# A graph-attention and mixture-of-experts layer: the vector a loaded as two rows and spread by a product with ones, and six products on constants at the start

## The chip, the cores and the metric

The kernel runs on one core of a Trainium2 chip. The metric is the time of one execution on the device in microseconds (us), median over several executions. A core has five engines with an instruction queue each: TensorE (PE; its weight loads are shown apart as PEld), VectorE (DVE), ScalarE (ACT), GpSimd (POOL) and SyncE (SP). SP here only issues DMA transfers; ACT issues two at the start. All transfers share 16 DMA engines.

## What is computed

One layer on x of 3327 x 256, padded to 3328 rows: graph attention with 4 heads of 64 columns over a random adjacency matrix, then a mixture of 16 experts of which each row takes two. Cut to what matters here:

```
h = (layernorm(x) @ W).reshape(n, 4, 64)
a1, a2 = a[:64, 0], a[64:, 0]
s = einsum('nhd,d->nh', h, a1 + a2)
e = where(adj[:, None, :] > 0, leaky_relu(s)[:, :, None], -9e15)
h' = einsum('nhm,mhd->nhd', softmax(e), h)
x = x + layernorm(h') * gamma + beta
x = x + mixture_of_experts(layernorm(x))
```

The vector `a` has 128 values, and it is used through the sum of its two halves alone.

## The kernel before

**Score columns.** The scores s are linear in the rows of h, so four columns are put in front of W: `w_sb` has `H + D` = 260 columns, the first four being W of each head times `a1 + a2`, summed over the 64 columns. `score_columns` makes them on VectorE: `a_sum` from the two halves of `a_bc` (L457), the product `ha` with W (L459), and the sums (L461). `a_bc` is `a` broadcast to all 128 partitions by a DMA on ScalarE's queue (`row_broadcast`, L222, called at L242). W follows on the same queue (L244).

**Centring.** The layer norm's mean is taken out of W in place of x: `center` multiplies W by a constant matrix `mean` on TensorE (L447) and subtracts the result on VectorE (L450), once for the 256 columns of W, once for the four score columns.

**The h stage.** The 26 row tiles (128 rows each) are in seven groups (`SIZES`). For each tile `h_stage` takes statistics of x on VectorE (L492, L493), the root on GpSimd (L497, L498), turns the tile by two transposes on TensorE (L473), copies it on ScalarE (L476, tile `xnt`), multiplies it by `w_sb` (L481), and splits the result into a high part on ScalarE (`hi`, L484) and a low part on VectorE (`lo`, L487). Group 0 is loaded in four tiles, the others group by group (`load_x`, L240).

**The masks.** Blocks of the adjacency matrix of up to 512 x 512 are loaded (`sg`, L561), turned into ones and zeros on VectorE (`mk`, L564) and multiplied with hi and lo on TensorE (L587, L588). There are three buffers for blocks and three for masks.

**After that** each group is finished (softmax terms, layer norms, routing), and the experts work on gathered rows (L959, L974, L985), whose results are added to the output (L988).

**The order.** Nearly all work is given to `plan`. Each `plan.add` names an engine, an assumed cost in us, a rank, what it comes after, the buffers that it uses, and for a load an assumed time to landing and a size. `Plan.run` makes 80 orders by a greedy choice (the work that can start earliest by the assumed times, then the rank), replays each with random variations of the costs, and emits the one with the smallest total. Every engine then works in that order. What stands above the plan in the code (constants, the loads of `a` and W) is emitted first, in the order of the code. PSUM buffers are named by a kind and the rest of a key: the kinds `pt` and `ph` have two buffers each, and a new key waits for the users of the key two before it.

The works that open the plan are at L1080 to L1089: four loads of x tiles, the landing of W (a work without an instruction), `score_columns`, and the two centrings.

Of the kernel before, what the change touches and what calls it, by code (L numbers as in the profile page):

```python
# [47 lines left out]
F32 = mybir.dt.float32  # L48
# [6 lines left out]
P = 128  # L55
# [3 lines left out]
D = 256  # L59
H = 4  # L60
DH = 64
# [15 lines left out]
CAP = 512  # L77
# [137 lines left out]
def gnn_moe(ctx: ExitStack, tc: tile.TileContext, x, adj_t, W, a, gamma, beta, gate_w, gate_b, w1, w2, w3, out):  # L215
    nc = tc.nc

    const = ctx.enter_context(tc.tile_pool(name="const", bufs=1))

    def row_broadcast(ap, size, name):  # L220
        t = const.tile([P, size], F32, name=name)
        nc.scalar.dma_start(t, bass.AP(tensor=ap.tensor, offset=ap.offset, ap=[[0, P], [1, size]]))  # L222
        return t


    XF = [const.tile([P, len(tiles), ROW], F32, name=f"x{g}") for g, tiles in enumerate(GROUPS)]
    X = [t[:, :, :D] for t in XF]
# [2 lines left out]
    def row_of(t):  # L230

        return (t + FIRST) % NT * P
# [5 lines left out]
    def load_x(g, t0, t1):  # L238
        r0 = row_of(GROUPS[g][0]) + t0 * P
        nc.sync.dma_start(X[g][:, t0:t1, :], x[r0:r0 + (t1 - t0) * P, :].rearrange("(t p) d -> p t d", p=P))  # L240

    a_bc = row_broadcast(a, 2 * DH, "a_bc")  # L242
    w_sb = const.tile([P, KC, H + D], F32, name="w_sb")
    nc.scalar.dma_start(w_sb[:, :, H:], W.rearrange("(k p) d -> p k d", p=P))  # L244
    gamma_bc = const.tile([P, D], F32, name="gamma_bc")
# [12 lines left out]
    ones = const.tile([P, P], BF, name="ones")  # L258
# [5 lines left out]
    warm = const.tile([P, 1], F32, name="warm")  # L264
# [72 lines left out]
    tiny = ctx.enter_context(tc.tile_pool(name="tiny", bufs=2))  # L337
# [10 lines left out]
    PE, DVE, ACT, POOL, SP = "PE", "DVE", "ACT", "POOL", "SP"  # L348
# [51 lines left out]
    plan = Plan(SLOTS, take)  # L400
# [7 lines left out]
    def psum(key):  # L408
        return T[key]
# [31 lines left out]
    SPLIT, LOADED = {}, {}  # L441
# [11 lines left out]
        return means, subtract  # L453

    def score_columns():
        a_sum = tiny.tile([P, DH], F32, name="a_sum", bufs=1)
        nc.vector.tensor_add(a_sum, a_bc[:, :DH], a_bc[:, DH:])  # L457
        ha = work.tile([P, KC, H, DH], F32, name="ha", bufs=1)
        nc.vector.tensor_tensor(ha, w_sb[:, :, H:].rearrange("p k (h d) -> p k h d", h=H),  # L459
                                a_sum[:, None, None, :].to_broadcast([P, KC, H, DH]), op=ALU.mult)  # L460
        nc.vector.tensor_reduce(w_sb[:, :, :H], ha, AX.X, ALU.add)  # L461
# [615 lines left out]

    for t in range(GT):  # L1080
        LOADED[0, t] = plan.add(SP, 0.6, (0, t), [], lambda t=t: load_x(0, t, t + 1), landing=2.0, size=P * D * 4)

    landed = plan.add(SP, 0.0, (0, 0), [], lambda: None, landing=2.5, size=D * D * 4)
    summed = plan.add(DVE, 1.6, (0,), [landed], score_columns)
    SCORES = []
    for made, c0, c1, c in ((landed, H, H + D, 1.0), (summed, 0, H, 0.5)):
        means, subtract = center(w_sb, ("ph", "w", c0), c0, c1)
# [4 lines left out]
    for step in range(NG):  # L1092
        if step + 1 < NG:
            g = step + 1
            LOADED[g] = plan.add(SP, 0.6, (1, step - 0.5), [], lambda g=g: load_x(g, 0, len(GROUPS[g])), landing=2.0,
                                 size=len(GROUPS[g]) * P * D * 4)
# [46 lines left out]
    size = 3 * D * HID * 4  # L1143
# [22 lines left out]
    with tc.If(many["value"] > 0):  # L1166
        with tc.For_i(0, NL) as i:
# [4 lines left out]
            with tc.For_i(0, full * (NT // AGAIN)) as c:  # L1172
# [12 lines left out]
                for k in range(KC):  # L1185
                    pt = ps_tr.tile([P, CAP], F32, name="pt")
# [51 lines left out]
```

## Time and profile before

| | us |
|---|---|
| median of 3 runs | 533.23 (532.13 to 533.85) |
| the profiled execution | 530.4 |
| its span, first to last instruction | 528.7 |
| VectorE starts on x | 5.37 |
| first product with W (L481) starts | 10.91 |
| first mask product (L587) starts | 14.77 |
| last product (L985) is done | 522.7 |

All times in the text are from the start of the span. DMA issues are on the queue of the engine that issues them (ACTq, SPq): the time shown there is the issuing, not the transfer. From 5 to 30 us the DMA engines move 317 to 386 GB/s, and nearly nothing from 31 to 45 us. From 15 us to 200 us PE shows no idle time. A group of instructions in the trace is shown with its start, its whole length and its count; matmuls are pipelined, so a group's length over its count comes nearer to what one costs than a single one's shown duration.

### The profile page before, as it was taken

To read this page: it belongs to the slowest core of one execution; us is meant where nothing else is said; L and a number is where in the kernel's file an instruction comes from. 1 tells how busy PE (TensorE), PEld (TensorE's weight loads), DVE (VectorE), ACT (ScalarE), POOL (GpSimd) and SP (SyncE) were. 2 spreads that over 40 slices of the span, in tenths; PEclk is the share of its full clock that TensorE was granted. 3 is DMA by queue.
4 is the path that set the end of the run, shared out by engine and by line. 5 is a ranking of instruction groups with operands and counts; after the bars stand their busy time and mean duration, and the time that the engine had idled before them with its cause. 6 is when DMAs were issued, how large, how long until landed. Compare 5 with 4: busy or idle time off the path is not lost. (4 is left out here: it accounts for less than half of the span.)

```text
span 528.7 us, 8608 instructions
## 1 busy us (share of the span) xinstructions
PE 513.8 (97%) x2997; PEld 406.5 (77%) x2998; DVE 274.5 (52%) x848; ACT 161.2 (30%) x464; POOL 213.0 (40%) x240
## 2 busy tenths in 40 slices
PE   5999999999999999999899999999999999999995
PEld 4889999999999999777687557566566756666673
DVE  4978564876869799678822222222233233423221
ACT  2562153636372750565222211201211121112110
POOL 4230022121031411756676555364465546622333
PEclk9999999999999999999999999999999999999999
DMA  7932889797879895554649544463465545543222
GB/s 269 366 128 75 304 261 300 247 338 230 273 212 360 271 374 168 184 153 136 173 83 304 150 96 125 107 147 116 112 143 154 136 111 140 152 109 68 30 29 28
DMA packets 63534, 94.69 MB, mean 179 GB/s; under 512 B 4858, under 2 KB 36990, under 8 KB 63488
## 3 DMA queue, kind: packets, MB, share of 16 engines
q1 hardware_dynamic: 52304, 80.04, 46.2%
q0 software_dynamic: 10768, 13.75, 15.3%
q8 instruction: 24, 0.39, 0.3%
q10 hardware_dynamic: 416, 0.33, 0.2%
q14 instruction: 22, 0.18, 0.1%
HBM read 81.61 MB, written 13.90 MB: 181 GB/s over the span
## 5 line engine op out<-in xcount | busy, mean ns | idle before, releaser
L587 PE MATMUL pa<-hi,mk 128*128 128x258 f32 x676 | 167.6, 289 | 0.0
L588 PE MATMUL pa<-lo,mk 128*128 128x256 f32 x676 | 163.2, 281 | 0.0
L587 PEld LDWEIGHTS pa<-hi,mk 128*128 128x128 f32 x676 | 127.7, 189 | 1.1 <-issue 1.0
L588 PEld LDWEIGHTS pa<-lo,mk 128*128 128x128 f32 x676 | 127.5, 189 | 0.1
L988 POOL DMA_INDIRECT out<-y,out_index x61 | 94.0, 1541 | 60.7 <-DVE y L1068 38.9
L974 PE MATMUL pa<-xt,w1e 128*128 128x400 f32 (+8 forms) x272 | 98.6, 485 | 0.0
L974 PE MATMUL pa<-xt,w2e 128*128 128x400 f32 (+8 forms) x272 | 98.0, 483 | 0.0
L1050 DVE TENSOR_TENSOR hid<-s,pa 128x400 f32<-128x400 f32 (+9 forms) x76 | 40.3, 530 | 109.2 <-PE pa L974 89.2
L959 POOL DMA_INDIRECT x<-normed,index x61 | 64.1, 1050 | 81.3 <-PE pt L1030 59.0
L1047 ACT ACTIVATE s<-pa 128x400 f32<-128x400 f32 (+9 forms) x76 | 35.8, 472 | 196.9 <-PE pa L974 196.9
L985 PE MATMUL ph<-w3e,hid 128*128 128x256 f32 (+2 forms) x400 | 89.4, 379 | 0.0
L985 PEld LDWEIGHTS ph<-w3e,hid 128*128 128x128 f32 (+2 forms) x400 | 73.7, 188 | 10.4
L974 PEld LDWEIGHTS pa<-xt,w2e 128*128 128x128 f32 x272 | 49.5, 190 | 36.9 <-issue 18.0
L974 PEld LDWEIGHTS pa<-xt,w1e 128*128 128x128 f32 x272 | 49.2, 190 | 35.7 <-issue 19.8
L564 DVE TENSOR_SCALAR mk<-sg 128x2048 fp32r<-128x2048 f32 (+2 forms) x49 | 54.2, 1107 | 28.6 <-PE pa L588 28.6
L1068 DVE TENSOR_SCALAR y<-ph,weight 128x256 f32<-128x256 f32 (+5 forms) x54 | 26.0, 482 | 70.5 <-PE ph L985 64.2
L653 POOL TENSOR_TENSOR hp<-csum,c 128x512 f32<-128x512 f32 (+1 forms) x14 | 15.1, 1097 | 65.0 <-DVE c L649 65.0
L481 PE MATMUL ph<-w_sb,xnt 128*128 128x260 f32 x104 | 27.6, 401 | 0.0
L1037 ACT COPY xt<-pt 128x512 f32<-128x512 f32 (+2 forms) x38 | 17.4, 504 | 19.4 <-PE pt L1030 19.4
L481 PEld LDWEIGHTS ph<-w_sb,xnt 128*128 128x128 f32 x104 | 18.2, 193 | 4.0 <-issue 1.2
L423 POOL TENSOR_SCALAR rs_x<-spread_x 128x4 f32<-128x4 f32 (+1 forms) x7 | 1.8, 259 | 47.4 <-ACT pay L429 44.3
L667 ACT ACTIVATE agg<-agg,c 128x64 f32<-128x64 f32 x76 | 18.8, 336 | 1.9 <-DVE c L649 1.8
(177 smaller groups left out, 466.3 us busy)
## 6 DMA issues: line engine op xcount, KB each, us to landing
sg<-in_adj_t SPq DMA_DIRECT2D x25, 1024.0 KB, 6.1
sg<-in_adj_t SPq DMA_DIRECT2D x20, 768.0 KB, 5.0
w1e<-in_ffn_w SPq DMA_DIRECT2D x15, 512.0 KB, 3.3
w2e<-in_ffn_w SPq DMA_DIRECT2D x15, 512.0 KB, 4.4
w3e<-in_ffn_w SPq DMA_DIRECT2D x15, 512.0 KB, 4.5
normed<-pay SPq DMA_DIRECT2D x5, 520.0 KB, 6.6
out<-x SPq DMA_DIRECT2D x5, 512.0 KB, 5.6
sg<-in_adj_t SPq DMA_DIRECT2D x4, 576.0 KB, 4.6
```

Source lines behind the costliest of these rows:

```text
L481: nc.tensor.matmul(ph[:, :H + D], T["xnt", g, t][:, k, :], w_sb[:, k, :], start=(k == 0), stop=(k == KC - 1))
L564: nc.vector.tensor_scalar(T[mk][:, :m, :n * P], T[sk][:, :m, :n * P], 0.0, None, op0=ALU.is_gt)
L587: nc.tensor.matmul(pa[:, :D + 2], lhs, HI[mg][:, i, H:], start=first, stop=False)
L588: nc.tensor.matmul(pa[:, :D], lhs, LO[mg][:, i, H:], start=False, stop=left[g, t] == 0)
L667: nc.scalar.mul(at, at, some("c")[:, 0, t, h:h + 1])
L959: nc.gpsimd.indirect_dma_start(out=xe[:, t, :], out_offset=None, in_=normed[:limit], in_offset=at_rows(idx, t), bounds_check=limit - 1, oo ...
L974: nc.tensor.matmul(p[:, :n], wt[:, k, j * P:(j + 1) * P], xt[:, k, :n], start=(k == 0), stop=(k == KC - 1))
L985: nc.tensor.matmul(py[:m, :D], hid[:, j, t * P:t * P + m], w3e[:, j, :], start=(j == 0), stop=(j == JC - 1))
L988: i = nc.gpsimd.indirect_dma_start(out=out, out_offset=at_rows(idx, t, m), in_=y[:m], in_offset=None, bounds_check=NP - 1, oob_is_err=Fals ...
L1047: nc.scalar.activation(T["gate", i, j][:, :n], psum(key)[:, :n], AF.Silu)
L1050: nc.vector.tensor_mul(hid()[:, j, :n], T["gate", i, j][:, :n], psum(key)[:, :n])
L1068: nc.vector.tensor_scalar(T[yk][:mm], psum(key)[:mm, :D], weight, None, op0=ALU.mult)
```

## The change

The broadcast load of `a` goes. In its place SP loads `a` as two rows of 64 values, `a_rows`, just after the first tile of x, and a product of a `[2, 128]` tile of ones, `two`, with `a_rows` puts the sum of both halves into all 128 partitions of a PSUM tile (`("ph", "a")`). `score_columns` reads that tile; its addition goes. Before everything else on TensorE stands `warm_up`: six products of the constant bf16 tile `ones` with itself, repeated to 512 columns, into a `pt` tile that nobody reads. The planned costs of the first x loads go from 0.6 to 0.45, and that of `score_columns` from 1.6 to 1.4.

```
-    def row_broadcast(ap, size, name):
-        t = const.tile([P, size], F32, name=name)
-        nc.scalar.dma_start(t, bass.AP(tensor=ap.tensor, offset=ap.offset, ap=[[0, P], [1, size]]))
-        return t
...
-    a_bc = row_broadcast(a, 2 * DH, "a_bc")
+    a_rows = const.tile([2, DH], F32, name="a_rows")
+    two = const.tile([2, P], F32, name="two")
+    nc.vector.memset(two, 1.0)
...
     def score_columns():
-        a_sum = tiny.tile([P, DH], F32, name="a_sum", bufs=1)
-        nc.vector.tensor_add(a_sum, a_bc[:, :DH], a_bc[:, DH:])
+        a_sum = psum(("ph", "a"))[:, :DH]
...
+    def warm_up():
+        for _ in range(6):
+            nc.tensor.matmul(psum(("pt", "warm")), ones, ones[:, None, :].to_broadcast([P, CAP // P, P]), start=True, stop=True)
+
+    plan.add(PE, 2.2, (0, -1), [], warm_up, [("pt", "warm")])
     for t in range(GT):
-        LOADED[0, t] = plan.add(SP, 0.6, (0, t), [], lambda t=t: load_x(0, t, t + 1), landing=2.0, size=P * D * 4)
+        LOADED[0, t] = plan.add(SP, 0.45, (0, t), [], lambda t=t: load_x(0, t, t + 1), landing=2.0, size=P * D * 4)
+        if t == 0:
+            got = plan.add(SP, 0.45, (0, t), [], lambda: nc.sync.dma_start(
+                a_rows, bass.AP(tensor=a.tensor, offset=a.offset, ap=[[DH, 2], [1, DH]])), landing=2.0, size=512)
+
+    spread = plan.add(PE, 0.2, (0,), [got], lambda: nc.tensor.matmul(psum(("ph", "a"))[:, :DH], two, a_rows, start=True, stop=True),
+                      [("ph", "a")])
 
     landed = plan.add(SP, 0.0, (0, 0), [], lambda: None, landing=2.5, size=D * D * 4)
-    summed = plan.add(DVE, 1.6, (0,), [landed], score_columns)
+    summed = plan.add(DVE, 1.4, (0,), [landed, spread], score_columns, [("ph", "a")])
```

## The prediction

> **What bounds the kernel now.** The page comes first: its busy times, and the span cut into slices of 13.2 us.
>
> ```profile
> PE 513.8 (97%) x2997; PEld 406.5 (77%) x2998; DVE 274.5 (52%) x848; ACT 161.2 (30%) x464; POOL 213.0 (40%) x240
> PE   5999999999999999999899999999999999999995
> PEclk9999999999999999999999999999999999999999
> ```
>
> PE is busy nearly throughout, and only the first and the last slice hold half a slice of idle time. So a microsecond by which PE begins its stream sooner, or runs it faster, moves the end unless a new wait eats it. The PEclk digits cannot show a slow clock inside the first slice.
>
> Second, the waits of PE over the whole span (total us, times, longest):
>
> ```profile
> PE pt L473 <- DMA x<-in_x: 5.5, 1, 5.5
> PE pt L1030 <- DMA x<-normed,index: 1.4, 1, 1.4
> PE ph L447 <- DMA w_sb<-in_gnn_W: 0.9, 1, 0.9
> ```
>
> Two of the three large ones are at the start: for the first tile of x, then for W. Nothing large stands between there and 262 us, where the 1.4 us are.
>
> Third, PE in order of time from 5 to 24 us (start, length of the group, line, tiles, count):
>
> ```profile
> 5.48 0.66 PE L473 MATMUL pt<-ident,x 128*128 128x128 f32 x2 [5.48 <-DMA x<-in_x]
> 7.05 2.05 PE L447 MATMUL ph<-w_sb,mean 128*128 128x256 f32 x4 [0.91 <-DMA w_sb<-in_gnn_W]
> 8.89 1.06 PE L473 MATMUL pt<-ident,x 128*128 128x128 f32 x4
> 9.74 0.85 PE L447 MATMUL ph<-w_sb,mean 128*128 128x4 f32 x4
> 10.91 2.44 PE L481 MATMUL ph<-w_sb,xnt 128*128 128x260 f32 x8
> ...
> 17.26 0.60 PE L473 MATMUL pt<-ident,x 128*128 128x128 f32 x4
> ...
> 19.88 2.02 PE L481 MATMUL ph<-w_sb,xnt 128*128 128x260 f32 x8
> ```
>
> Compare like with like. Four transposes take 1.06 us at 8.89 and 0.60 at 17.26. A 256-column f32 product takes 0.51 at 7.05 (2.05 over 4), a 260-column one 0.25 at 19.88 (2.02 over 8), and the eight at 10.91 are in between. TensorE runs its first work at half speed and speeds up during the eight products that begin at 10.91.
>
> Fourth, ScalarE's queue and VectorE over the same stretch:
>
> ```profile
> 0.83 0.40 ACTq L222 DMA_DIRECT2D a_bc<-in_gnn_a  x1
> 1.27 0.46 ACTq L244 DMA_DIRECT2D w_sb<-in_gnn_W  x1
> ...
> 5.93 0.19 DVE L457 TENSOR_TENSOR a_sum<-a_bc 128x64 f32<-128x64 f32 x1
> 7.01 0.69 DVE L459 TENSOR_TENSOR ha<-w_sb,a_sum 128x512 f32<-128x512 f32 x1 [0.89 <-DMA w_sb<-in_gnn_W]
> 7.74 0.69 DVE L461 TENSOR_REDUCE w_sb<-ha 128x8 f32<-128x512 f32 x1
> 9.13 0.69 DVE L450 TENSOR_TENSOR w_sb<-w_sb,ph 128x512 f32<-128x512 f32 x1 [0.71 <-PE ph L447]
> 10.63 0.16 DVE L450 TENSOR_TENSOR w_sb<-w_sb,ph 128x8 f32<-128x8 f32 x1 [0.26 <-PE ph L447]
> 13.10 0.49 DVE L487 SCALAR_TENSOR_TENSOR lo<-ph,rs,hi 128x260 fp32r<-128x260 f32 x1 [0.16 <-ACT hi L484]
> 13.50 1.22 DVE L564 TENSOR_SCALAR mk<-sg 128x2048 fp32r<-128x2048 f32 x1
> ```
>
> a is not what is late: its sum is done at 6.12, and the next instruction then waits 0.89 us for W. The chain runs from W's landing (about 6.9) through ha, the reduction, the two centrings (the first of which waits 0.71 us for the slow means) to the first product at 10.91. Then come hi, lo and the first mask (13.50 to 14.72), and PE's first mask product at 14.77.
>
> **The change, part by part.** *The broadcast of a goes.* It has 64 KB and stands ahead of W on ScalarE's queue. W is issued at 0.83 in place of 1.27, 0.44 us sooner. The 64 KB themselves are 0.20 us at the 317 GB/s that the DMA engines moved from 5 to 7 us. W, which lands 5.6 us after its issue, so comes between 0.20 us (bytes alone) and 0.64 us (bytes and issue) sooner. I take 0.45, near the middle because both act on the same queue: W at 6.45.
>
> *The two rows of a* go out on SP behind the first tile of x. SP's first issues take 2.30 us for five, 0.46 each, so the three other tiles, group 1 and the first adjacency block leave 0.46 later. The rows land between 2.3 us (issue at 1.29, plus the 1 us after which the first bytes of any load moved) and 6.3 us (the 5.0 us that a's broadcast took). A 512-byte transfer behind one tile is nearest to that tile, which took 4.5: 5.8. SP's later loads move too. Group 2 goes out at 5.83 now, just when a has landed (0.83 plus 5.0); if it waits for the oldest load afterwards, it waits for W, 0.6 us longer. That is hidden: the first adjacency block is in flight until 3.17 plus 8.6, 11.8 us.
>
> [...]
>
> *The product with ones* is two PE instructions (an f32 product is issued as two: the four means of L447 are two slices of W). The nearest row is 9.74, 0.85 over 4, so 0.21 each: 0.43 slow, half that fast. It goes behind the first transposes, about 5.9 to 6.4, in the idle time before W. Without this cover, with a at 6.3, the means of W would wait behind it on PE until about 6.9, which costs 0.4.
>
> *a_sum on VectorE* (0.19) goes, at nothing: it lies in the wait for W. ha then reads PSUM; L450, of the same size with a PSUM operand, takes 0.69 like ha now, so zero. The added memset (0.06, by neg_half's of 128x4) delays ones at 0.93 by as much, long before anything is due.
>
> *The six products on constants.* 512 bf16 columns have no row. A 256-column mask product follows the one before by 0.12 us at 19 us; twice that is 0.24, and six are 1.4 us fast, 2.8 slow. I take 2.8, since all early rows are slow: PE is busy from about 1.2 to 4.0, all before x lands at 5.4, so they cost nothing themselves. What they buy lies between nothing and all of the slow rows' excess: 1.05 in the means of W (2.05 less 4 times 0.25), 0.46 in the transposes, 0.43 in the 4-column means (taken as half of 0.85), 0.4 in the first product (four at 1.4 less 1.0), 2.3 in all. I take the fast clock by 8.5 us or sooner, since PE then has 2.8 us of work before x and is dense again from 6.5.
>
> [...]
>
> **The sum along the chain.** W 6.45; ha and reduction (0.69 each and the gaps) to 7.9. The means, fast, end at 7.6, so the first centring no longer waits: 7.9 to 8.6. Transposes and small means lie beside it, to 8.6. The statistics that stand between the centrings (0.42 and 0.18) and the second centring end at 9.4; first product at 9.45 in place of 10.91, 1.45 sooner; with its own 0.4 it ends 1.85 sooner. If the clock rises only at 8.5, the means end at 8.6 and the first centring at 9.3; the first product then starts 0.7 later, at 10.1, and its end is 1.2 sooner. Late next is the mask: its block lands at 11.8 (0.2 sooner by bytes, 0.46 later by SP's shift: 11.6 to 12.3), while the conversion could start at 13.50 less 1.85, 11.65. By the mask the gain is 1.2 to 1.85. Further masks have the same slack: blocks land at 6.24 plus 9.7, 15.9, and 11.85 plus 9.3, 21.2, and are converted at 17.53 and 22.64. The x loads have more. I take 1.85, as PE's tail is dense and its products are not all behind the masks; 1.2 is the low end. The profiled execution was 530.4 us (span 528.7) and would become 528.5. It lies 2.8 below the median; the same shift on the median gives 533.23 - 1.85 = 531.4.
>
> **Rivals.** *The clock stays low until about 12 us*: the warm-up is too short, or the 1.4 us of idle time after it undo it, so that part of the change does not do what it says. Only W's 0.45 is left: 532.8. For it: the slow rows last 4.8 us from 7.05 in spite of work from 5.48. Against it: the constants add more than half as much work again.
>
> *PE is not held by the masks*: all of W's best 0.64 and the 2.3 arrive, 2.9: 530.3. For it: PE has other work to order in; against: VectorE is busy 4.82 of 5 us from 15 to 20.
>
> *Slower, by the planner's order.* Costs and works at the start change, so the planner chooses a new order for every engine. Place: VectorE's queue from 13 to 25 us, busy 4.8 of 5. If conversions move one block ahead (four statistics, 4 times 0.53, 2.1 us) while blocks land no sooner, each waits 1.85 + 2.1 less the slack of 1.6, 2.3 us, with lo products queued behind that PE needs. One such move cancels the gain; two give 533.23 - 1.85 + 4.6 = 536.0. It decides from 1.85 us of such waits on. For it: conversions wait for nothing today but their slack is only 1.5 us. Against: planned costs hardly change.
>
> **How the numbers follow.** Forecast 0.50 (531.4, own range 530.6 to 532.2), low clock 0.25 (532.8), everything arrives 0.13 (530.3), slower 0.12. Change of under 0.3%, 1.6 us, is about what a measurement of this kernel can tell from none: 531.6 to 534.8. The forecast lies just below that edge; 0.37 of its 0.50 and the third case give 0.50 faster; 0.38 same; 0.12 slower. Range: from 530.3 less half a microsecond of scatter (the three runs span 1.7) to the low clock plus as much, 529.8 to 533.4; the slower case stays outside.
>
> **What would show it.** Right: the first means row with about 0.25 per product instead of 0.51, W about 6.45, the first product near 9.5, the first mask product near 13. Wrong on the clock: 0.51 there and products slow until 12. Wrong on the masks: VectorE waiting for sg. Wrong altogether: PE gaps over 0.5 us beyond 15 us that are not there now.

## The result, and the profile after

The changed kernel takes 532.14 us (median of 6 runs, 531.49 to 534.65), the kernel before in the same session 533.32 (532.13 to 533.85): a ratio of 0.9986, with a 95% interval of 0.9963 to 1.0008. These runs alone do not tell it from no change. Two later sets of runs, told below, gave 0.9982 (0.9967 to 0.9996) and 0.9964 (0.9951 to 0.9976). So the change makes the kernel faster, by 0.14 to 0.36% at the medians of the three sessions, 0.75 to 1.9 us. Its profiled execution took 532.32 us, with a span of 530.6.

The first view of the changed kernel is its page: the busy times, and PE's busy tenths and granted clock in 40 slices of the span.

```profile
PE 517.0 (97%) x3005; PEld 406.5 (77%) x3006; DVE 274.1 (52%) x848; ACT 160.8 (30%) x464; POOL 213.3 (40%) x240
PE   8999999999999999999898999999999999999995
PEclk9999999999999999999999999999999999999998
```

The first slice has gone from 5 tenths to 8. PE is busy 3.2 us more in all, of which 2.74 are the six products on constants, and the share of the span is the same 97%. As before, the clock digits do not show the slow start; it is read from what single products take.

The second view is PE in order of time (start, length of the group, line, tiles, count; in brackets the idle time before it and what ended it).

```profile
1.28 2.74 PE L1080 MATMUL pt<-ones 128*128 128x512 bf16 x6 [1.28 <-DVE neg_half L259]
3.82 0.63 PE L470 MATMUL pt<-ident,x 128*128 128x128 f32 x2
4.38 0.66 PE L1089 MATMUL ph<-a_rows,two 2*128 2x64 f32 x2
4.97 1.13 PE L445 MATMUL ph<-w_sb,mean 128*128 128x256 f32 x4
...
7.73 2.02 PE L478 MATMUL ph<-w_sb,xnt 128*128 128x260 f32 x8
...
12.62 0.39 PE L584 MATMUL pa<-hi,mk 128*128 128x258 f32 x1 [1.01 <-DVE mk L561]
...
22.90 2.13 PE L478 MATMUL ph<-w_sb,xnt 128*128 128x260 f32 x8 [0.34 <-DVE lo L484]
```

The wait for x is gone: x's first tile landed at 3.54 (5.34 before) and is turned at 3.82 (5.48 before). The wait for W is gone too. The four means take 1.13 us here and 2.05 before, so the clock was already raised at 5 us (the trace records the full clock from 4.9 us on here, from 11.9 in the first profile of the kernel before). The first product with W starts 3.18 us sooner. But the first mask product starts only 2.15 us sooner, after an idle microsecond that was not there before. At 22.90 there is another short wait. VectorE, in the same form, says for what:

```profile
5.08 0.69 DVE L456 TENSOR_TENSOR ha<-w_sb,ph 128x512 f32<-128x512 f32 x1 [0.86 <-PE ph L1089]
...
11.34 1.23 DVE L561 TENSOR_SCALAR mk<-sg 128x2048 fp32r<-128x2048 f32 x1 [1.15 <-DMA sg<-in_adj_t]
...
15.47 1.23 DVE L561 TENSOR_SCALAR mk<-sg 128x2048 fp32r<-128x2048 f32 x1
...
21.10 1.23 DVE L561 TENSOR_SCALAR mk<-sg 128x2048 fp32r<-128x2048 f32 x1 [0.42 <-DMA sg<-in_adj_t]
```

The conversions of the first and of the third block of adj now wait for their loads. The block, not the chain through W, sets when the masks begin. ha waits for the spread a, no longer for W.

The gain is 2.15 us at the first mask product and 1.5 us from 30 us on (1.54 at the 51st product with W, in a table below), and yet this span is 1.9 us longer than the 528.7 of the profile before. The windows of the two traces say where (from and to, length, PE busy and its instructions, granted clock, DMA share, GB/s; the clock column, too, says nothing of the slow start). First the kernel before:

```profile
0.00:25.00 25.00, 18.59 (x91) 1.00 0.93 314
25.00:216.00 191.00, 191.00 (x1609) 1.00 0.76 249
...
276.00:292.00 16.00, 16.00 (x92) 1.00 0.89 274
```

Then the changed kernel:

```profile
0.00:25.00 25.00, 22.18 (x106) 1.00 0.93 315
25.00:216.00 191.00, 191.00 (x1616) 1.00 0.76 249
...
276.00:292.00 16.00, 14.05 (x78) 1.00 0.81 240
```

From 25 to 216 us PE has no idle time in either, so a lead at 25 us is carried on whole. Between 276 and 292 us PE idles for 2 us in the changed kernel and not at all in the profiled execution of the kernel before. Whether the change does that is the first question for the experiments.

### The profile page after: what moved, and what is told of

It is laid out like the page before. It is cut to its first block, busy times and chain, and to the rows that moved or that the text cites. A ratio compares the mean times of both kernels' runs of the same rounds, so it can differ in the third digit from the quotient of the medians.

```text
span 530.6 us, 8626 instructions
## 1 busy us (share of the span) xinstructions
PE 517.0 (97%) x3005; PEld 406.5 (77%) x3006; DVE 274.1 (52%) x848; ACT 160.8 (30%) x464; POOL 213.3 (40%) x240
## 5 line engine op out<-in xcount | busy, mean ns | idle before, releaser
L1027 PEld LDWEIGHTS pt<-ident,x 128*128 128x128 f32 x122 | 14.3, 141 | 7.1 <-issue 6.1
```

## The experiments

All were timed against the kernel before, in three sessions of four runs after the session of the result, each on another chip. Its median was 533.12 us in the first, 530.76 in the second, 531.30 in the third, so only ratios are compared across sessions. At the start three theories stood. **A**: the loss at 276 to 292 us comes and goes with executions and has nothing to do with the change. **M**: the start is gained, but the landings of the blocks of adj cap it. **C**: the raised clock carries the gain. The planner's order, a rival of the prediction, needed no run: instruction by instruction each engine's order is the same before and after, but for the works that were added and removed.

### The two kernels again, and each part alone

The first two runs are the kernel before and the changed kernel as they are.

> The kernel before, unchanged, once more. Theory A (the start gives PE about 1.5 us for good, and the 3 us that the profile of the changed kernel loses to the one of before from 276 to 290 us belong to single executions, not to the change): time within 0.1% of before; its profile has a span nearer to 531 than to 528.7 us, and set against the first profile of before it loses 1 to 3 us somewhere after 250 us. Rival B (the profile of before is typical, and the change itself causes the stall from 276 to 290 us): span 528.5 to 529 us, PE within 0.5 us of the first profile all along. In both the first tile of x lands at 5.3 us and W at 6.9 if the late landings belong to the kernel; at 3.5 and 4.5 if they belong to that execution.

> The changed kernel, unchanged, once more. Theory A: 0.9970 to 0.9985 of before; first product with W at 7.5 to 8.5 us, the first mask product at 12.5 to 13.2, PE 1.3 to 1.8 us ahead of before at 200 us; no stall of 3 us between 276 and 290 us, or one at another place. Rival B: the same start, and the stall from 276 to 290 us again, so that the span is again 1 to 2 us longer than 528.7.

The third is the changed kernel without its warm-up, the fourth the kernel before with the warm-up alone:

```diff
-    plan.add(PE, 2.2, (0, -1), [], warm_up, [("pt", "warm")])
```

```diff
+    plan.add(PE, 2.2, (0, -1), [], warm_up, [("pt", "warm")])
```

> The changed kernel without the six products on constants. If the products raise the clock: it now rises only at 8 to 12 us, the first means row takes 0.5 us per product again, the first product with W starts 1.5 to 2.5 us later than in the changed kernel (9.3 to 10.3 us), and PE at 50 us is 0.3 to 0.9 us ahead of before, not 1.5; time 0.9985 to 0.9995 of before. If the two rows alone carry the gain: first product near 8.5, PE 1.5 us ahead at 50 us, time like the changed kernel's.

> The kernel before with the six products on constants put in front; a is still broadcast by the DMA. If the clock carries the gain: clock up at about 5 us, W still at 6.5 to 7 us, first product with W at 9.3 to 9.8, and as the first mask's block lands at 11.3 to 11.8 us in any case, the first mask product at 12.7 to 13.2: PE 1.2 to 1.5 us ahead at 50 us, time 0.997 to 0.9985 of before. If the early W is needed as well: PE only 0.5 to 0.9 us ahead at 50 us.

Measured: before again 0.9997 (0.9985 to 1.0009), after again 0.9982 (0.9967 to 0.9996), rows only 1.0000 (0.9983 to 1.0017), warm-up only 1.0002 (0.9989 to 1.0016). Starts in the first profile of each kernel and in these four, in us, read from the traces:

| kernel | x's first turn | first means of W | first product with W | first mask product | 51st product with W | last down product | span |
|---|---|---|---|---|---|---|---|
| before, first profile | 5.48 | 7.05 | 10.91 | 14.77 | 28.88 | 522.3 | 528.7 |
| before again | 5.42 | 7.02 | 10.55 | 14.20 | 28.30 | 525.2 | 531.5 |
| after, first profile | 3.82 | 4.97 | 7.73 | 12.62 | 27.34 | 524.3 | 530.6 |
| after again | 3.90 | 5.10 | 9.00 | 12.61 | 28.77 | 525.1 | 531.4 |
| rows only | 4.00 | 5.21 | 9.10 | 13.42 | 28.19 | 523.7 | 530.1 |
| warm-up only | 5.34 | 6.96 | 10.76 | 14.41 | 28.51 | 524.7 | 531.0 |

Theory A holds in this: the change is not the cause of the loss. The same windows of the kernel before, run again, show the loss:

```profile
0.00:25.00 25.00, 18.58 (x93) 1.00 0.94 315
25.00:216.00 191.00, 191.00 (x1612) 1.00 0.76 249
...
276.00:292.00 16.00, 14.50 (x86) 1.00 0.80 231
```

PE idles there in front of products of the experts, and the trace names nothing that it waits for:

```profile
282.37 0.71 PE L974 MATMUL pa<-xt,w1e 128*128 128x128 f32 x4 [0.44 <-issue]
...
284.58 0.71 PE L974 MATMUL pa<-xt,w1e 128*128 128x128 f32 x4 [0.65 <-issue]
```

The changed kernel run again had 14.65 of 16 us busy there, and 16.00 in the third session. ScalarE's 464 instructions have the same order in all traces, so each trace can be set against the first profile of the kernel before, instruction by instruction (us; a lead is how much sooner the instruction of 214 us comes, a loss what is lost from there to 301 us):

| session | kernels | lead at 214 us | lost from 214 to 301 us |
|---|---|---|---|
| of the result | after | 1.52 | 3.5 |
| first | before, after, rows only, warm-up only | 0.59, 0.13, 0.67, 0.35 | 3.5, 2.8, 2.0, 2.8 |
| second | the four told below | -0.38 to 1.92 | 0.7 to 1.0 |
| third | the four told below | 0.12 to 1.71 | 0.4 to 1.1 |

So the loss is up to 3.5 us, more than the change moves at the start, and it goes mostly with the session, not with the kernel: the session with losses of 2.0 to 3.5 us is also the one in which the kernel before took about 2 us longer than in the two after it. The first profile of the kernel before, at 530.4 us against a median of 533.23, was an execution without it. What brings it on stays open.

Three things follow from PE's order in the changed kernel run again:

```profile
1.28 2.74 PE L1080 MATMUL pt<-ones 128*128 128x512 bf16 x6 [1.28 <-DVE neg_half L259]
...
5.10 2.08 PE L445 MATMUL ph<-w_sb,mean 128*128 128x256 f32 x4
...
9.00 2.20 PE L478 MATMUL ph<-w_sb,xnt 128*128 128x260 f32 x8
...
12.61 0.39 PE L584 MATMUL pa<-hi,mk 128*128 128x258 f32 x1
```

First, the same six products did not raise the clock this time: the means take 2.08 us, half speed, and the full clock is on record only from 9.5 us on. Second, with the first product with W 1.27 us later than in the first profile of the same code, the first mask product starts at the same 12.6. Here nothing waits for the block: it landed at 11.22, and its conversion starts at 11.34, right behind the low part on VectorE. In the first profile the chain was a microsecond early and waited for the block (1.15 us). So what the raised clock won at 7.73 was waited off in front of the first mask: that speaks for M and against C. Third, rows alone brings W's means forward about as much as both parts do, and the warm-up alone does not move x or W: they come sooner because the broadcast is gone, not because of the constants.

Several expectations were missed. The changed kernel run again had its first product with W at 9.00, not by 8.5, was not 1.3 to 1.8 us ahead at 200 us, and had the loss again. Rows only was expected at 0.9985 to 0.9995 or at the changed kernel's time and showed no gain, with runs from 531.06 to 535.09 us. The warm-up alone was expected to raise the clock by 5 us and to gain; it did neither.

In the profile of the changed kernel run again, the rest of the lead goes at the third block. VectorE there:

```profile
22.53 1.23 DVE L561 TENSOR_SCALAR mk<-sg 128x2048 fp32r<-128x2048 f32 x1 [1.96 <-DMA sg<-in_adj_t]
```

Here the third block came 1.4 us later than in the first profile, VectorE waited 1.96 us, and PE stood 1.87 us for lo behind it. The lead at the 51st product with W is gone (28.77 against 28.30 to 28.88 in the kernel before). This profile is not typical, though: its execution, at 533.11 us, was the slowest of the twelve (median 532.17).

### What in the broadcast was dear

The prediction gave W 0.45 us for the removal; the traces show it landed at 4.2 to 4.5 in place of 6.8 to 6.9, about 2.4 sooner (its first means start 1.8 to 2.1 sooner), and x's first tile, which was given nothing, is turned 1.3 to 1.7 sooner. Two runs tell apart why. Both are the changed kernel with an unused load of 64 KB issued ahead of W, once the old broadcast of one row of a, once the first 512 bytes of 128 rows of W:

```diff
+    nc.scalar.dma_start(unused, bass.AP(tensor=a.tensor, offset=a.offset, ap=[[0, P], [1, 2 * DH]]))
```

```diff
+    nc.scalar.dma_start(unused, W[:P, :2 * DH])
```

> The changed kernel, with the old broadcast load of a to 128 partitions issued again by ACT ahead of W into a tile that nothing reads; the scores still come from a_rows and the product. Theory B (the 128 broadcast rows themselves, on the DMA engines, are what held x's first tile and W in the kernel before): x's first tile lands at 5.0 to 5.4 us and W at 6.5 to 6.9 (3.5 to 3.9 and 4.2 to 4.5 without the load), the first means of W start at about 6.9, and the time goes back by about 0.5 to 1.0, to 532.7 to 533.2. Rival (only the issue of the load ahead of W cost, 0.45): W lands at 4.7 to 4.9, x's first tile stays at 3.5 to 3.9, and the time stays at 532.1 to 532.4.

> The changed kernel with an unused load of the same size and shape (128 rows of 512 bytes, issued by ACT ahead of W) whose rows are 128 different rows of W, not one row 128 times. If the repeated address makes the broadcast dear, x's first tile lands near 3.7 to 4.0 and W near 4.7 to 5.0, and the time is that of the changed kernel (532.1 to 532.5). If it is the 128 descriptors or their 64 KB, whatever they read, the landings are those of the run with the unused broadcast (5.0 to 5.4 and 6.5 to 6.9), and so is its time.

Measured on one chip: 1.0008 (0.9991 to 1.0026) with the broadcast, 0.9987 (0.9978 to 0.9996) with different rows. The issue of the unused load and its time from issue to landing in the trace, first with the broadcast:

```profile
L242 ACTq DMA_DIRECT2D unused<-in_gnn_a x1: 405/405/405, 0.8 to 0.8; - x1
...
DMA to landing us min/median/max: 4.4/4.4/4.4
```

Then with different rows:

```profile
L242 ACTq DMA_DIRECT2D unused<-in_gnn_W x1: 405/405/405, 0.8 to 0.8; - x1
...
DMA to landing us min/median/max: 2.5/2.5/2.5
```

The same shape, bytes, queue and issue take 4.4 us against 2.5. Around it, x's first tile takes 4.1 against 2.3, and W, issued behind it, as follows. With the broadcast:

```profile
L244 ACTq DMA_DIRECT2D w_sb<-in_gnn_W x1: 466/466/466, 1.3 to 1.3; - x1
...
DMA to landing us min/median/max: 4.8/4.8/4.8
```

With different rows:

```profile
L244 ACTq DMA_DIRECT2D w_sb<-in_gnn_W x1: 467/467/467, 1.3 to 1.3; - x1
...
DMA to landing us min/median/max: 2.8/2.8/2.8
```

The source is all that differs between the two. So the dear thing is 128 reads of the same 512 bytes, and the loads in flight beside them pay. That it is the repetition and not the place of a in memory is likely, not shown: the two rows of a landed at 3.4 to 4.4 us in all profiles that load them. The difference is no scatter of landings: in the five profiles with a broadcast of a, x's first tile landed at 4.9 to 5.4 and W at 6.1 to 6.9, in the nine without it at 3.2 to 3.9 and 4.1 to 4.5. Why the repeated reads are slow, the traces do not say. The landings with the broadcast were a little under those expected (W at 6.1, not 6.5), those with different rows sooner than expected (W at 4.1, not 4.7), which makes the difference no smaller. The time follows, narrowly: the medians are 0.95 us apart, and when the 23 single times are dealt out at random the means lie that far apart in about 1 case of 100, though the two intervals overlap between 0.9991 and 0.9996. The profile with different rows does not help here: its execution was the slowest of its eleven, the first block came late, at 13.1 us, and its first mask product was at 14.37.

### More warm-up

```diff
-        for _ in range(6):
+        for _ in range(11):
```

> The changed kernel with 11 warm-up products in place of 6, 4.7 us of them from 1.3 to about 6.0. Theory M (the first masks and the third block's landing set the start, not the clock): the first products with W come with a raised clock (0.12 us each or so) and start at about 8, yet the first mask product stays at 12.5 to 12.7 us, and the time stays within 0.5 of the changed kernel's 532.2. Rival C (the clock, raised early in only one of three profiles of six products, is what the rest of the gain waits for): the time falls by 0.7 or more, to 531.5 or less. Should the longer warm-up stand in the way of the turns of x and W's means, the time rises to 532.5 to 533.

Measured: 0.9991 (0.9982 to 1.0001), 530.39 us, in the session where the two kernels above had 1.0008 and 0.9987. PE and then VectorE of this run:

```profile
1.28 4.87 PE L1080 MATMUL pt<-ones 128*128 128x512 bf16 x11 [1.28 <-DVE neg_half L259]
...
7.12 1.18 PE L445 MATMUL ph<-w_sb,mean 128*128 128x256 f32 x4
...
9.89 2.02 PE L478 MATMUL ph<-w_sb,xnt 128*128 128x260 f32 x8 [0.25 <-DVE w_sb L448]
```

```profile
7.23 0.69 DVE L456 TENSOR_TENSOR ha<-w_sb,ph 128x512 f32<-128x512 f32 x1 [2.77 <-PE ph L1089]
...
12.26 1.22 DVE L561 TENSOR_SCALAR mk<-sg 128x2048 fp32r<-128x2048 f32 x1
...
23.02 1.23 DVE L561 TENSOR_SCALAR mk<-sg 128x2048 fp32r<-128x2048 f32 x1 [1.53 <-DMA sg<-in_adj_t]
```

The clock is up for the means (on record from 7.3 us on), but ha waits 2.77 us for the spread of a, which stands behind the constants on PE, and the third block is late again. This execution, too, was the slowest of its twelve. The first product with W comes at 9.89, not at the 8 of theory M, and the first mask conversion no longer waits for its block. C's gain does not come. Neither expectation was met in its details: the price of the longer warm-up hid the cap that M was to show.

### The third block sooner

If the third block's landing takes the lead away, the loads in front of it may be to blame: gamma, beta and the gate, 280 KB, stand between group 3 of x and that block. The first instruction that reads any of them starts at 44 us.

```diff
-    rest = plan.add(SP, 2.0, (1, 1.5), [], load_rest, landing=2.0, size=2 * P * D * 4)
+    rest = plan.add(SP, 2.0, (1, 6.5), [], load_rest, landing=2.0, size=2 * P * D * 4)
```

> The changed kernel with the loads of gamma, beta and the gate's weights (280 KB) put behind the third block of adj and x's groups 2 to 4. Theory M: the third block lands at 19.8 to 20.5 us (21.1 to 22.5 with the loads in front), the wait for it on DVE and PE's gap of 0.6 to 2.2 us at 22 us go, the products lie 0.6 to 2 us sooner from there on, and the time falls by 0.5 to 1.5, to 530.7 to 531.7. Rival: other transfers stand behind in its place (x's groups, the fourth block), PE loses the same time between 22 and 35 us, and the time stays at 532.0 to 532.4 or rises.

Measured: 0.9973 (0.9963 to 0.9984), the lowest of its session. The planner also reorders some products and statistics around 20 us for it. The third session put it beside the changed kernel on one chip, and took it into the kernel before and into rows only.

> The changed kernel once more, as the measure for the three runs beside it: 0.997 to 0.999 of the kernel before, the third block of adj landing at 21 to 23 us with a gap of 0.6 to 2.2 us on PE there.

> The changed kernel with the 280 KB of gamma, beta and gate behind the third block, again, now on one chip with the changed kernel. If the third block's landing holds what was won at the start, it lands at 19.4 to 20.5 us, and the time lies 0.4 to 1.0 us under the changed kernel's (0.9960 to 0.9975 of the kernel before). If the 0.9973 of its first run was the chip's, it equals the changed kernel's within 0.2 us.

> The kernel before with the same one move (the 280 KB behind the third block), a broadcast to 128 partitions and no warm-up. If the move pays by itself, 0.9985 to 0.9992. If it only pays once the start is sooner (in the kernel before, the third block landed at 21.1 and PE had no gap over 0.5 us there), 0.9995 to 1.0005.

> The changed kernel without its warm-up, with the 280 KB behind the third block. If the sooner landings of x and W (no broadcast) and of the third block are what counts, 0.9970 to 0.9985, within 0.4 us of the run with the warm-up. If the warm-up carries a part of its own, 0.9985 to 1.0000, at 0.6 us or more above that run.

| third session | ratio to before (95%) | third block converted | 51st product with W | PE busy 0 to 25 us |
|---|---|---|---|---|
| changed kernel | 0.9964 (0.9951 to 0.9976) | 21.94 | 28.18 | 22.84 |
| changed, rest later | 0.9966 (0.9953 to 0.9979) | 19.70 | 26.85 | 23.46 |
| before, rest later | 1.0005 (0.9997 to 1.0014) | 21.36 | 28.52 | |
| rows only, rest later | 0.9975 (0.9962 to 0.9988) | 19.80 | 26.98 | |

VectorE of the changed kernel in that session, and then of the version with the rest later:

```profile
21.94 1.23 DVE L561 TENSOR_SCALAR mk<-sg 128x2048 fp32r<-128x2048 f32 x1 [0.94 <-DMA sg<-in_adj_t]
```

```profile
19.70 1.19 DVE L561 TENSOR_SCALAR mk<-sg 128x2048 fp32r<-128x2048 f32 x1
```

The landing is as expected, a little sooner: the block is there at 19.3, nothing waits for it, and the 51st product is 1.3 us sooner in these two profiles. The time does not show it: 529.49 against 529.50 us, 5 runs each. The profiled execution of the changed kernel, at 530.70 us, was the slowest of its five, and the first profile, without a late third block, has 27.34 there, so much of the difference is between executions. Waits of 0.94 us and more for the third block (0.94, 1.53, 1.96) stand in three profiles, each of them the slowest execution among its runs; how often a typical execution waits there is not shown. The version with the rest later is not shown to beat the changed kernel. In the kernel before the move brings nothing.

One thing stays untested here. The loads that were moved include three more broadcasts of one row to 128 partitions (gamma, beta and the gate's bias). Without them in front, the third block landed at 19.3 to 19.8 in place of 21.1 to 22.5, more than the 0.7 to 0.9 us that 280 KB take at 317 to 386 GB/s; SP also issues it about 4 us sooner. Which of these counts, no run tells apart.

### The two parts, pair by pair

Runs of one session that differ in one part alone say what each part is worth (difference of the medians, us):

| what is changed | in which kernel | us |
|---|---|---|
| broadcast to two rows | with the constants (warm-up only to changed kernel again) | -1.10 |
| broadcast to two rows | without (before again to rows only) | -0.17 |
| broadcast to two rows | without, rest later | -1.66 |
| constants added | with the broadcast (before again to warm-up only) | +0.16 |
| constants added | with two rows (rows only to changed kernel again) | -0.77 |
| constants added | with two rows, rest later | -0.22 |

With the constants, and with the rest later, the two rows are worth 1.1 and 1.7 us; in the latter pair the intervals are far apart (1.0005, from 0.9997 to 1.0014, against 0.9975, from 0.9962 to 0.9988). The pair with -0.17 has the rows-only runs that scatter over 4 us. No pair shows a gain of the constants that stands clear of the noise: the -0.77 has those same runs in it. The unused broadcast, put in against different rows, cost 0.95 us. So the removal of the broadcast carries the gain.

## Why the prediction was right, and where not

**The sign and, roughly, the size** hold: forecast 531.4, 1.85 us under the median before; measured 1.2 in the session of the result, 0.95 and 1.8 in the first and third sessions after it. The terms under it hold less well. Of the signs that the prediction named for being right, the fast means came (in the first profile) and the first mask near 13 (12.62); W at 6.45 and the first product near 9.5 did not (4.24 and 7.73). Its sign for being wrong on the masks, VectorE waiting for sg, came as well (1.15 us). So did its sign for being wrong altogether, PE gaps over 0.5 us beyond 15 us: 1.02 us at 282 us in the first profile, a place where the kernel before has such gaps in other executions, and 1.87 us at 24 us when it was run again, for the third block.

**W sooner by 0.45 (bounds 0.20 and 0.64)** is the term that was mis-sized: it measured about 2.4, outside both bounds. The step behind it priced the broadcast by its bytes at 317 GB/s and by its issue. The runs show that neither gives its price: 128 different rows with the same bytes and issue leave W at 4.1 us, 128 times one row holds it until 6.1. The same error gave x's first tile nothing; it came 1.3 to 1.7 us sooner.

**The two rows of a** were taken to land at 5.8, as the tile beside them; they landed at 4.0 to 4.4 in the changed kernel, and at 3.9 even in the run with the unused broadcast, where that tile came at 4.9. The tile was the wrong yardstick. Their semaphore shows two landings (3.84 and 3.96 in the first profile) where the tile's shows sixteen. **The product with ones** was hidden by the wait for W. That cover went with the broadcast: ha waits 0.86 us for the product in the first profile, 0.44 to 2.77 in others, while W has landed at 4.2 to 4.5. The prediction named this case, but priced it by a late a; what came late was PE behind its transposes (the wait is 0.78 us in rows only, without any constants). ha reading PSUM at 0.69 and a_sum at nothing were right.

**The warm-up with a raised clock by 8.5** was right in the first profile and not as a rule. Of eight profiles with six products, two have fast means of W (1.13 us for four), six slow ones (2.04 to 2.08). The traces record the full clock from 4.1 and 4.9 us on in those two and from 9.1 to 11.9 in the six, as late as in the five without constants (9.1 to 11.9). The products took 2.74 us, close to the 2.8 predicted. That they would have the clock up by 8.5 was the author's estimate. No run shows how much work the clock asks for, or why two executions had it early and six did not: the full clock that is on record at 4.1 us (the first run with the rest later) came 2.8 us after the first product, the one at 4.9 us 3.6 us after it. In the one profile with 4.87 us of constants it came at 7.3, 6.0 us after the first product.

**The masks as the low end** were right: the first block landed at 11.2 to 11.8 in all profiles but three (10.9 twice, 13.1 once), forecast 11.6 to 12.3, and the conversion started at 11.34, 11.34 and 11.68, forecast 11.65. But only the fast-clock profiles reach this end by the predicted way: there W's extra 2 us and the clock's 2.3 together run into the load. In the slow-clock profiles W's extra 2 us stood in for the clock that did not come, and the chain reached the first mask about when its block did (11.34 against 11.22, 11.68 against 11.61). That these two errors cancel is luck. **The same slack for further masks** was wrong at the third block: forecast to land at 21.2 and converted at 22.64 before, it had less slack (1.4) than the 1.85 taken from it, and it came as late as 22.5; VectorE waited 0.42, 1.96 and 0.94 us for it in the three profiles of the changed kernel.

**The rivals.** The low clock did come true in most profiles. Its price of 532.8 rested on W's 0.45, which was too small; the measured 532.14 lies midway between it and the forecast, so the time does not tell the two apart. "Not held by the masks" did not happen. The planner's order did not change. What stays open is the warm-up's own share: without it, rows only stood at 1.0000 against 0.9982 in one session, and 0.9975 against 0.9966 with the rest later in another; in both the intervals overlap.

## What to carry to other kernels

A small load that is broadcast to all partitions at the start of a kernel can cost far more than its bytes: here 128 reads of one row took 1.9 us more than reads of 128 rows, and the loads beside them paid too, where two rows and a product with ones cost PE 0.66 us. When the first work is freed, look at once for the load that is late next: here blocks of adj that, in the changed kernel, land at 11.2 to 11.6 and at 21.1 to 22.5 us. Six warm-up products (2.74 us) had the clock up early in two profiles of eight; eleven (4.87 us) had it up at the means in the one profile taken, but stood in the way of the first real product. A wait in a profile that shows the slowest of several executions need not be typical: three such profiles had the longest waits for the third block.

## What the runs showed of the hardware

VectorE began on x's first tile only behind the last of the load's sixteen landings: the first and the last were 2.79 and 3.54 us in the first profile of the changed kernel, 2.85 and 5.34 in that of the kernel before, and VectorE began at 3.57 and 5.37. In the run with different rows a single packet of 1 KB took 1.8 us at 5.8 us (the next longest between 5.4 and 6.4 us took 0.35), and from there on every load's last landing lay 3.2 to 3.9 us behind its first up to 20 us, where it had been 0.3 to 1.3 until then. Whether that packet is the cause, and on which engine it ran, the traces do not say.

On one kernel the profiled executions differ by up to 2.8 us in span (528.7 and 531.5 for the kernel before, in two sessions). From 214 to 301 us the second loses 3.5 us on the first, most of it at 276 to 292 us, where PE idles for reasons that the profile does not name; such losses were 2.0 to 3.5 us in the first session of experiments and at most 1.1 in the two after it. A comparison of two single profiles would have shown this change as a loss.
